# A relational graph network with attention: layers two and three gather three bf16 parts of each row instead of fp32 rows

## The chip, the cores and the metric

The kernel runs on one core of one Trainium2 chip. The metric is the device time of one execution in microseconds (us); of several runs the median is given. All engine times below come from one profiled execution.

A core has five engines with a queue of instructions each. TensorE multiplies matrices (PE in the profile; PEld is its loading of weights). VectorE (DVE) and ScalarE (ACT) work on elements. GpSimd (POOL) is used here almost only to issue gathers. SyncE (SP) issues ordinary DMAs. Each engine works through its queue in order and waits on semaphores for the others.

## The reference

A graph has 6250 nodes with 256 features and 100,000 edges (`src`, `dst`, sorted by `dst`), each with one of eight types. Three relational layers are followed by one attention layer, each of the two blocks with a residual and a layer norm:

```python
edge_index = jnp.stack([src, dst])
for l in range(3):                                   # relational block
    xr = jnp.einsum('nd,rde->rne', x, W_rel[l])      # 8 x 6250 x 256
    msg = xr[edge_type, src]
    agg = jax.ops.segment_sum(msg, dst, num_segments=x.shape[0])
    x = jax.nn.relu(agg + x @ W_root[l] + bias[l])
x = layernorm(x_in + x)
# attention block: logits from x @ weight, softmax over the heads, then
x = layernorm(x + attention(x))
```

All inputs and the output are fp32. The destinations are drawn as the square of a uniform number, so low node numbers have many more edges than high ones.

## The kernel before, in words

**Sums before weights.** A layer sums the raw rows of the source nodes first, separately for each destination node and edge type, and multiplies the sums with the eight weight matrices afterwards. Edges are cut into 782 tiles of 128. The first 36 tiles, whose destinations are the lowest nodes, are treated in another way (`count` and `products`); the other 746 tiles are gathered in every layer.

**Groups.** `Plan.order` puts the 746 tiles into 188 groups of four (three groups have two) and deals them to two streams, f = 0 for the high edge tiles and f = 1 for the low ones, mostly taking turns. Each stream runs from high nodes to low ones and has a ring `S[f]` in SBUF: four node tiles of 128 columns for f = 0, three for f = 1, for each of two feature halves and eight types.

**An iteration** of the loop in `layer` (L778) handles one group, in an order that is written out by hand:

- `gather` (L492) issues four indirect DMAs on POOL (L496). Each fetches 128 rows of 1 KB from the table of the layer into a tile `msg`. The pool `mp` has eight such buffers. The table of layer one is the input, those of layers two and three are `xs[1]` and `xs[2]` in DRAM.
- `onehot` (L476) makes, four groups ahead, the 0/1 matrix `oh` on VectorE (L480): for each edge, 1 in the column of its destination and type. `w` is eight times the width of the group's window of nodes, from 32 to 208 columns.
- `finish` (L593) handles a node tile whose products are done: VectorE adds the bias (L595), ScalarE applies the relu (L598), SP stores the rows to `xs[l + 1]` (L599). In the last layer it continues with residual and layer norm. `clear` (L589) then zeroes the tile's columns in the ring on ScalarE.
- `windows` (L501) multiplies `msg` with `oh` on TensorE, two products per edge tile (one for each half of the features), into a PSUM tile `pw` (L513). There are four such banks.
- Pieces of `dense` (L572) come next: two root products (L577) and sixteen relation products (L581) per node tile, all fp32, six of them in an iteration for each node tile in progress.
- `add` (L518) adds each window from PSUM into the ring at the place of its nodes (L525), on VectorE.
- A node tile whose last group has come is folded (L557, L559) and queued for `dense`. Tile 13 gets edges from both streams. Its sums from stream 1 are copied to `hold[13]` by `keep` (L565, ScalarE) and added later to the ring of stream 0 by VectorE (L824).

**Other work in the loop.** In layer one, from iteration 56, `count` (L633) makes two selection matrices an iteration on VectorE (L647) for the hot nodes. From iteration 130 `products` (L663) loads all rows again in tiles `msg`. In layer three `logits` (L619) transposes each finished tile and multiplies it, and from iteration 164 `prepare` (L703) readies the attention, also with tiles `msg`.

**The order of the layers.** A gather of a layer needs all rows of the layer before, so at each seam the last group, its dense products, the relu and the store all have to end before the first gather of the next layer starts. The weights of the next layer are loaded by ScalarE's queue at the same point (L228). `split3` (L877) is an existing helper that writes a tensor as three bf16 tensors with the same sum: a cast, a subtraction, a cast, a subtraction, a cast, on VectorE. It is used for two small tensors of the attention.

Of the kernel before, what the change touches and what calls it, by code (L numbers as in the profile page):

```python
# [20 lines left out]
P = 128  # L21
# [96 lines left out]
@with_exitstack  # L118
def kernel(
    ctx: ExitStack,  # L120
    tc: tile.TileContext,
    x: bass.AP,
    src: bass.AP,
    dst: bass.AP,
    edge_type: bass.AP,
    w_rel: bass.AP,
    w_root: bass.AP,
    bias: bass.AP,
    weight: bass.AP,
    attn_l: bass.AP,  # L130
    attn_r: bass.AP,
    out: bass.AP,
):
    nc = tc.nc
    N, D = x.shape
    E = src.shape[0]
    L, R = w_rel.shape[0], w_rel.shape[1]
    H, DH = attn_l.shape
    KC = D // P
    pl = Plan(N, E, R)  # L140
    NT, T, CH, WMAX = pl.NT, pl.T, pl.CH, pl.WMAX
    LAST = N - (NT - 1) * P
    assert R * WMAX * KC <= 512 and E >= NT * P and NT <= P

    const = ctx.enter_context(tc.tile_pool(name="const", bufs=1))
    dram = ctx.enter_context(tc.tile_pool(name="dram", bufs=1, space=DRAM))
    xs = [x] + [dram.tile([N, D], F32, name=f"x{l}") for l in range(1, L)]

    flag = const.tile([1, 1], I32, name="flag")

    fast(tc, const, pl, x, xs, src, dst, edge_type, w_rel, w_root, bias, weight,
         attn_l, attn_r, out, flag)

    bad = nc.values_load(flag[0:1, 0:1], min_val=0, max_val=6 * T)  # L154
    with tc.If(bad > 0):
        general(tc, x, src, dst, edge_type, w_rel, w_root, bias, weight, attn_l, attn_r, out)


def fast(tc, const, pl, x, xs, src, dst, edge_type, w_rel, w_root, bias, weight,
# [10 lines left out]
    with ExitStack() as top:  # L170
# [31 lines left out]
        with ExitStack() as s:  # L202
            wp = s.enter_context(tc.tile_pool(name="wp", bufs=1))
            sp = s.enter_context(tc.tile_pool(name="sp", bufs=1))
            mp = s.enter_context(tc.tile_pool(name="mp", bufs=8))
# [10 lines left out]
            hold = {j: sp.tile([P, KR, P], F32, name=f"hold{j}") for j in sorted(pl.shared(pl.TM))}  # L216
# [23 lines left out]
            with tc.manual_schedule():  # L240
                for l in range(L):
                    wr, wo = load_w(l)
                    opn = layer(
                        tc, pl, l, l == L - 1, groups, ready, S, hold, A, hk, hl, idx, key, pos,
                        iota, ident, wr, wo, bias_b, x, xs, eps, w1x, altab, y,
                        (al3, ga, hif, yT0, lane, dst, iota_p),
                        mp, op, xp, hp, ps_w, ps_d, ps_t, H)
# [194 lines left out]
def fold_weights(tc, mp, w1x, weight, attn_l, attn_r):  # L442
# [6 lines left out]
    for i, a in enumerate((attn_r, attn_l)):  # L449
        t = mp.tile([P, GT, D], F32, name="msg")  # L450
        ab, pr = t[:, 0], t[:, 1:1 + KC]
        nc.sync.dma_start(ab, a.rearrange("h d -> (h d)").partition_broadcast(P))
        nc.vector.tensor_tensor(pr, w1x[:, :, :D], ab.unsqueeze(1).to_broadcast([P, KC, D]),
                                ALU.mult)
        for k in range(KC):
            nc.vector.tensor_reduce(w1x[:, k, D + i * H:D + (i + 1) * H],
                                    pr[:, k].rearrange("p (h d) -> p h d", h=H), AX.X, ALU.add)


def layer(tc, pl, l, final, groups, ready, S, hold, A, hk, hl, idx, key, pos, iota, ident, wr, wo,  # L460
          bias_b, x, xs, eps, w1x, altab, y, att, mp, op, xp, hp, ps_w, ps_d, ps_t, H):
# [14 lines left out]
    def onehot(i):  # L476
        g = groups[i][1]
        w = R * pl.W[g[0] // WB]
        oh = op.tile([P, GT, R * pl.WMAX], F32, name="oh")
        nc.vector.tensor_tensor(  # L480
# [11 lines left out]
    def gather(i):  # L492
        g = groups[i][1]
        msg = mp.tile([P, GT, D], F32, name="msg")
        for q, t in enumerate(g):
            nc.gpsimd.indirect_dma_start(  # L496
                out=msg[:, q, :], out_offset=None, in_=table,
# [3 lines left out]
    def windows(i, msg, oh):  # L501
# [6 lines left out]
        for n, (q, t) in enumerate(reversed(list(enumerate(g)))):  # L508
# [3 lines left out]
            for k in range(KC):  # L512
                nc.tensor.matmul(pw[:, k * w:(k + 1) * w], msg[:, q, k * P:(k + 1) * P],  # L513
                                 oh[:, q, :w], start=True, stop=True)
# [50 lines left out]
    def keep(j):  # L565

        i = nc.scalar.copy(hold[j], cols(1, j))
        tc.add_to_no_dep_group(f"used{l}_1_{j}", i.ins)
        done[1].append(j)
        clear(1, j)  # L570

    def dense(f, j, xT):  # L572
# [3 lines left out]
        for k in range(KC):  # L576
            nc.tensor.matmul(pd[:, :D], xT[:, k], wo[:, k], start=(k == 0), stop=False)  # L577
            yield
        for k in range(KC):
            for r in range(R):  # L580
                i = nc.tensor.matmul(pd[:, :D], s[:, k * R + r], wr[:, k, r],  # L581
                                     start=False, stop=(k == KC - 1 and r == R - 1))
# [10 lines left out]
    def finish(j, pd):  # L593
        n = rows(j)
        nc.vector.tensor_tensor(pd[:, :D], pd[:, :D], bias_b[:, l], ALU.add)  # L595
        if not final:
            h = xp.tile([P, D], F32, name="h", bufs=2)
            nc.scalar.activation(h, pd[:, :D], AF.Relu)  # L598
            nc.sync.dma_start(xs[l + 1][j * P:j * P + n, :], h[:n])  # L599
            return  # L600
# [13 lines left out]
        yt = xp.tile([P, D], F32, name="yt", bufs=2)  # L614
# [48 lines left out]
    def products():  # L663
# [4 lines left out]
        def load(js):  # L668
            t = mp.tile([P, GT, D], F32, name="msg")
# [33 lines left out]
    def prepare():  # L703
# [8 lines left out]
        for m in range(len(parts) + 2):  # L712
            todo = []
            if m < len(parts):
                js = parts[m]
                t = mp.tile([P, GT, D], F32, name="msg")
# [12 lines left out]
            if m >= 2:  # L729
                js = parts[m - 2]  # L730
                t = mp.tile([P, GT, D], F32, name="msg").rearrange("p a d -> p (a d)")
# [46 lines left out]
    for i in range(NG + 5):  # L778
# [18 lines left out]
        for f, j, pd in fin:  # L797
            yt = finish(j, pd)
            clear(f, j)
            if final:  # L800
                log.append((i, (j, yt)))
# [16 lines left out]
        for f, j in sorted((k for k, r in ready.items() if r == i), key=lambda k: -k[1]):  # L818
            fold(f, j)
            if f == 1 and j in late:  # L820
                keep(j)
                continue
            if j in hold:
                nc.vector.tensor_tensor(cols(f, j), cols(f, j), hold[j], ALU.add)  # L824
            turned.append(dense(f, j, xTs.pop(j)))
# [507 lines left out]
```

## Time and profile before

| | |
|---|---|
| Median of 3 runs | 2999.32 us (2997.8 to 3003.55) |
| Profiled execution, its own time | 2994.72 us |
| Its span, first to last instruction | 2993.0 us |
| Mean granted TensorE clock | 0.933 |
| POOL busy | 2159.9 us, 2238 gathers of 0.95 us |
| PE busy | 2667.7 us |
| VectorE busy | 1667.6 us |
| Software DMA queue (the gathers) | 293.48 MB, 33.7% of the time of 16 DMA engines |

A busy share is an average over stages. An instruction that issues a DMA from SP or ACT doesn't count as busy, but an indirect gather on POOL does. "L513" is line 513 of the kernel. A row of the groups reads: line, engine, operation, output and inputs with the number of instructions; then busy time and the mean of one; then idle time of the engine just before them and what ended it. In the timeline a row gives start, time, engine, line, operation, and in brackets the idle time before it. An fp32 matmul appears as two records.

### The profile page before, as it was taken

The page shows a single profiled execution, that of the slowest core. Times are in us where ns is not written, and L with a number is a line of the kernel's source. Part 1 is how long each engine was busy: PE and PEld are TensorE (multiplying, and loading weights), DVE is VectorE, ACT ScalarE, POOL GpSimd, SP SyncE. Part 2 cuts the span into 40 slices and gives each one's busy share as a digit, 9 for nine tenths or more (in the row PEclk, how much of TensorE's full clock was granted, in tenths as well). Part 3 has the DMA queues.
Part 4 walks back from the last instruction along what each step waited for, and adds up shares of the span by engine and source line. Part 5 has one row for each costly group of instructions (what it writes and reads, how often), then busy time and mean ns, then how long its engine had stood idle before and what let it go on. Part 6 is the DMA issues. An engine that isn't in the chain of part 4 may idle for free. (4 is left out here: it accounts for less than half of the span.)

```text
span 2993.0 us, 45318 instructions
## 1 busy us (share of the span) xinstructions
PE 2667.7 (89%) x15710; PEld 2424.1 (81%) x15711; DVE 1667.6 (56%) x4106; ACT 462.6 (15%) x611; POOL 2159.9 (72%) x2258
## 2 busy tenths in 40 slices
PE   5999999999987799999998997789999999999874
PEld 4989888888876798998887887678888888898763
DVE  7655667754433555554444443355656655555775
ACT  2111111111001111111111010011111111111015
POOL 6777777777775777777777777577777777777723
PEclk9999999999878899999999997799999999999885
DMA  5444444445433344444434543344444444454634
GB/s 153 125 123 122 119 123 120 120 133 170 135 116 115 117 123 122 125 123 118 123 116 146 164 126 117 117 119 131 126 132 128 125 127 127 150 169 138 187 97 131
DMA packets 203053, 388.97 MB, mean 130 GB/s; under 512 B 42885, under 2 KB 128004, under 8 KB 202820
## 3 DMA queue, kind: packets, MB, share of 16 engines
q0 software_dynamic: 107424, 293.48, 33.7%
q1 hardware_dynamic: 87464, 85.04, 8.9%
q10 hardware_dynamic: 7932, 7.48, 0.7%
q8 instruction: 130, 2.13, 0.3%
q14 instruction: 103, 0.84, 0.1%
HBM read 360.18 MB, written 25.65 MB: 129 GB/s over the span
## 5 line engine op out<-in xcount | busy, mean ns | idle before, releaser
L496 POOL DMA_INDIRECT msg<-x,idx x1492 | 1419.2, 951 | 504.6 <-issue 411.9
L513 PE MATMUL pw<-oh,msg 128*128 128x160 f32 (+22 forms) x8952 | 1308.0, 303 | 195.6 <-DMA msg<-x,idx 101.4
L513 PEld LDWEIGHTS pw<-oh,msg 128*128 128x128 f32 x8952 | 1253.8, 202 | 261.2 <-issue 119.9
L525 DVE TENSOR_TENSOR S<-S,pw 128x320 f32 (+22 forms) x2238 | 904.5, 404 | 989.4 <-PE pd L581 508.1
L581 PE MATMUL pd<-wr,S 128*128 128x256 f32 x4704 | 1107.0, 385 | 1.7 <-DVE S L525 1.4
L581 PEld LDWEIGHTS pd<-wr,S 128*128 128x128 f32 x4704 | 893.1, 193 | 119.3 <-DVE S L525 3.6
L496 POOL DMA_INDIRECT msg<-in_x_dram,idx x746 | 709.0, 950 | 236.0 <-issue 210.8
L480 DVE TENSOR_TENSOR oh<-iota,key 128x640 f32<-128x640 f32 (+23 forms) x564 | 363.8, 647 | 26.4 <-issue 14.8
L590 ACT ACTIVATE S<-S 128x2048 uint32<-128x2048 uint32 x150 | 285.0, 1900 | 0.1
L551 ACT COPY xT<-pt 128x256 f32<-128x256 f32 x195 | 72.3, 371 | 972.6 <-PE pt L548 972.5
L598 ACT ACTIVATE h<-pd 128x256 f32<-128x256 f32 x98 | 37.7, 384 | 937.0 <-DVE pd L595 752.3
L577 PE MATMUL pd<-wo,xT 128*128 128x256 f32 x588 | 168.3, 412 | 3.3 <-ACT h L598 3.3
L595 DVE TENSOR_TENSOR pd<-pd,bias_b 128x256 f32<-128x256 f32 x147 | 63.1, 429 | 172.4 <-PE pd L581 172.3
L577 PEld LDWEIGHTS pd<-wo,xT 128*128 128x128 f32 x588 | 110.0, 205 | 13.1 <-ACT h L598 3.7
L647 DVE TENSOR_SCALAR sel<-iota,hk 128x392 bf16<-128x392 f32 x138 | 80.4, 613 | 0.0
L612 ACT ACTIVATE rs<-mv,eps 128x1 f32<-128x1 f32 x49 | 14.4, 295 | 413.1 <-DVE mv L611 413.1
L685 PE MATMUL pd<-msg,A 128*128 128x256 f32 x294 | 71.5, 386 | 1.5 <-DMA msg<-x 1.5
L1014 POOL TENSOR_TENSOR z<-yg,td 128x1536 f32<-128x1536 f32 (+1 forms) x9 | 29.3, 3268 | 56.7 <-DVE bn L992 28.0
L685 PEld LDWEIGHTS pd<-msg,A 128*128 128x128 f32 x294 | 55.7, 196 | 8.5 <-issue 1.8
L548 PE MATMUL pt<-ident,xin 128*128 128x128 f32 x294 | 57.4, 278 | 1.4 <-ACT xT L551 1.4
L629 PEld LDWEIGHTS pt<-w1x,xT 128*128 128x128 f32 x192 | 25.8, 195 | 35.2 <-ACT xT L551 35.2
L548 PEld LDWEIGHTS pt<-ident,xin 128*128 128x128 f32 x294 | 41.2, 145 | 12.7 <-ACT xT L551 2.4
(187 smaller groups left out, 669.4 us busy)
## 6 DMA issues: line engine op xcount, KB each, us to landing
msg<-x,idx POOLq DMA_INDIRECT x1492, 2.7
x<-h SPq DMA_DIRECT2D x96, 128.0 KB
xin<-x SPq DMA_DIRECT2D x96, 128.0 KB
msg<-x SPq DMA_DIRECT2D x24, 512.0 KB
msg<-in_x_dram,idx POOLq DMA_INDIRECT x746, 2.7
y<-yt SPq DMA_DIRECT2D x49, 128.0 KB
wr<-in_L_gnn_W_rel_dram ACTq DMA_DIRECT2D x6, 1024.0 KB
xin<-in_x_dram SPq DMA_DIRECT2D x48, 128.0 KB
```

The source lines that it names most:

```text
L480: nc.vector.tensor_tensor(oh[:, :len(g), :w], iota[:, :w].unsqueeze(1).to_broadcast([P, len(g), w]), key[:, g[0]:g[-1] + 1].unsqueeze(2).t ...
L496: nc.gpsimd.indirect_dma_start(out=msg[:, q, :], out_offset=None, in_=table, in_offset=bass.IndirectOffsetOnAxis(ap=idx[:, t:t + 1], axis=0))
L513: nc.tensor.matmul(pw[:, k * w:(k + 1) * w], msg[:, q, k * P:(k + 1) * P], oh[:, q, :w], start=True, stop=True)
L525: ins = nc.vector.tensor_tensor(o, o, pw.rearrange("p (a b) -> p a b", b=W), ALU.add)
L548: nc.tensor.transpose(pt[:, k * P:(k + 1) * P], t[:, k * P:(k + 1) * P], ident)
L551: nc.scalar.copy(xT.rearrange("p k n -> p (k n)"), pt[:, :D])
L577: nc.tensor.matmul(pd[:, :D], xT[:, k], wo[:, k], start=(k == 0), stop=False)
L581: i = nc.tensor.matmul(pd[:, :D], s[:, k * R + r], wr[:, k, r], start=False, stop=(k == KC - 1 and r == R - 1))
L590: i = nc.scalar.memzero(cols(f, j))
L595: nc.vector.tensor_tensor(pd[:, :D], pd[:, :D], bias_b[:, l], ALU.add)
L647: nc.vector.tensor_scalar(oh, iota[:, :NT * R], float(512 * n), hk[:, t:t + 1], op0=ALU.add, op1=ALU.is_equal)
L685: nc.tensor.matmul(ph[:, :D], A[:, j], t[:, n], start=(n == 0), stop=(j == js[-1]))
```

## The change

- **A second table.** Beside `xs[l]` there is `xb[l]` for layers two and three, with rows of 1536 bytes. `finish` of layers one and two splits the relu's result with `split3` into three bf16 parts, stored side by side, and stores the tile there with a further DMA on SP.
- **Gathers.** Layers two and three gather rows of `xb[l]`. The `msg` tile grows from 4 x 1 KB to 4 x 1.5 KB per partition, in all layers, and the pool `mp` has six buffers instead of eight.
- **Products of edge tiles.** In layers two and three `windows` runs three bf16 products, summed in PSUM, in place of each fp32 one. The one-hot matrix is written as bf16 there, in the same buffer. Layer one keeps fp32.
- **The shared node tile.** `keep` goes. Tile 13 now runs `dense` for stream 1 as well, without root products, and `finish` copies the result (256 columns) from PSUM to `hold[13]`. When stream 0 finishes the tile, this is added to its PSUM result. This holds for all three layers.

```diff
+    xb = [None] + [dram.tile([N, 3 * D // 2], F32, name=f"xb{l}") for l in range(1, L)]
...
-            mp = s.enter_context(tc.tile_pool(name="mp", bufs=8))
+            mp = s.enter_context(tc.tile_pool(name="mp", bufs=6))
...
-            hold = {j: sp.tile([P, KR, P], F32, name=f"hold{j}") for j in sorted(pl.shared(pl.TM))}
+            hold = {j: sp.tile([P, D], F32, name=f"hold{j}") for j in sorted(pl.shared(pl.TM))}
...
         oh = op.tile([P, GT, R * pl.WMAX], F32, name="oh")
+        if l:
+            oh = oh.rearrange("p g w -> p (g w)").bitcast(BF16)[:, :GT * R * pl.WMAX].rearrange(
+                "p (g w) -> p g w", g=GT)
...
-        msg = mp.tile([P, GT, D], F32, name="msg")
+        msg = mp.tile([P, GT, 3 * D // 2], F32, name="msg")
         for q, t in enumerate(g):
             nc.gpsimd.indirect_dma_start(
-                out=msg[:, q, :], out_offset=None, in_=table,
+                out=msg[:, q, :] if l else msg[:, q, :D], out_offset=None, in_=xb[l] if l else table,
...
             for k in range(KC):
-                nc.tensor.matmul(pw[:, k * w:(k + 1) * w], msg[:, q, k * P:(k + 1) * P],
-                                 oh[:, q, :w], start=True, stop=True)
+                if l == 0:
+                    nc.tensor.matmul(pw[:, k * w:(k + 1) * w], msg[:, q, k * P:(k + 1) * P],
+                                     oh[:, q, :w], start=True, stop=True)
+                    continue
+                m3 = msg[:, q].bitcast(BF16)
+                for c in range(3):
+                    nc.tensor.matmul(pw[:, k * w:(k + 1) * w],
+                                     m3[:, c * D + k * P:c * D + (k + 1) * P], oh[:, q, :w],
+                                     start=(c == 0), stop=(c == 2))
...
-    def keep(j):
-
-        i = nc.scalar.copy(hold[j], cols(1, j))
-        tc.add_to_no_dep_group(f"used{l}_1_{j}", i.ins)
-        done[1].append(j)
-        clear(1, j)
-
     def dense(f, j, xT):
...
-        for k in range(KC):
+        for k in range(KC if xT is not None else 0):
             nc.tensor.matmul(pd[:, :D], xT[:, k], wo[:, k], start=(k == 0), stop=False)
...
-    def finish(j, pd):
+    def finish(f, j, pd):
         n = rows(j)
+        if f == 1 and j in late:
+
+            nc.vector.tensor_copy(hold[j], pd[:, :D])
+            return
+        if j in hold:
+            nc.vector.tensor_tensor(pd[:, :D], pd[:, :D], hold[j], ALU.add)
         nc.vector.tensor_tensor(pd[:, :D], pd[:, :D], bias_b[:, l], ALU.add)
         if not final:
             h = xp.tile([P, D], F32, name="h", bufs=2)
             nc.scalar.activation(h, pd[:, :D], AF.Relu)
             nc.sync.dma_start(xs[l + 1][j * P:j * P + n, :], h[:n])
+            t = xp.tile([P, 3 * D // 2], F32, name="yt", bufs=2)
+            split3(nc, xp, t.bitcast(BF16).rearrange("p (c d) -> p c d", c=3), h)
+            nc.sync.dma_start(xb[l + 1][j * P:j * P + n, :], t[:n])
             return
...
             fold(f, j)
-            if f == 1 and j in late:
-                keep(j)
-                continue
-            if j in hold:
-                nc.vector.tensor_tensor(cols(f, j), cols(f, j), hold[j], ALU.add)
-            turned.append(dense(f, j, xTs.pop(j)))
+            kept = f == 1 and j in late
+            turned.append(dense(f, j, None if kept else xTs.pop(j)))
```

The helper that is called for the split, unchanged by the diff:

```python
def split3(nc, pool, o, v):

    r = pool.tile(list(v.shape), F32, name="rest", bufs=1)
    nc.vector.tensor_copy(o[:, 0], v)
    nc.vector.tensor_tensor(r, v, o[:, 0], ALU.subtract)
    nc.vector.tensor_copy(o[:, 1], r)
    nc.vector.tensor_tensor(r, r, o[:, 1], ALU.subtract)
    nc.vector.tensor_copy(o[:, 2], r)
```

## The prediction

> **What bounds the kernel now.** I read the page's busy shares and costliest groups first, then the stretches, then the timeline at the seams between layers.
>
> ```profile
> PE 2667.7 (89%) x15710; PEld 2424.1 (81%) x15711; DVE 1667.6 (56%) x4106; ACT 462.6 (15%) x611; POOL 2159.9 (72%) x2258
> L496 POOL DMA_INDIRECT msg<-x,idx x1492 | 1419.2, 951 | 504.6 <-issue 411.9
> ```
>
> TensorE looks like the bound and GpSimd (POOL) looks 28% free. The second line corrects that: a gather is 951 ns, and most of POOL's idle time is "issue", not a wait for another engine. The table of stretches settles it (columns: stretch; length; PE, PEld, DVE, ACT, POOL busy with counts; clock; DMA).
>
> ```profile
> 300.00:400.00 100.00, 94.39 (x566) 84.48 (x565) 71.39 (x162) 16.12 (x20) 75.63 (x81) 1.00 0.42 123
> 1100.00:1200.00 100.00, 97.44 (x556) 89.12 (x556) 53.19 (x105) 17.52 (x20) 75.63 (x81) 1.00 0.42 123
> 1800.00:1900.00 100.00, 83.96 (x443) 76.71 (x444) 34.42 (x101) 7.67 (x9) 76.21 (x79) 0.76 0.38 112
> ```
>
> PE goes from 97 to 84 busy and its clock from 1.00 to 0.76, while POOL stays near 76. In the timeline gathers start every 1.25 us: 0.95 of instruction and 0.30 between. A layer has 746 gathers, so 746 x 1.25 = 932 us, and the spans from first to last gather are 936.0, 935.3 and 947.6 us. **The pace of gathers is the bound**; PE is a close second that sets the time in three places only: where POOL waits for a message buffer that PE still reads, at the seams, and at the end. Counting matmuls against gathers in the timeline, the third layer loses 14.7 us to gathers that start late (PE runs up to seven groups behind there), the first 3.4 and the second 2.8.
>
> The seam between layers one and two:
>
> ```profile
> 946.02 0.95 POOL L496 DMA_INDIRECT msg<-in_x_dram,idx  x1 [0.31 <-issue]
> ...
> 953.61 7.17 PE L581 MATMUL pd<-wr,S 128*128 128x256 f32 x32
> 960.89 0.43 DVE L595 TENSOR_TENSOR pd<-pd,bias_b 128x256 f32<-128x256 f32 x1 [7.33 <-PE pd L581]
> 961.36 0.38 ACT L598 ACTIVATE h<-pd 128x256 f32<-128x256 f32 x1 [7.78 <-DVE pd L595]
> 967.16 0.94 POOL L496 DMA_INDIRECT msg<-x,idx  x1 [20.19 <-DMA wr<-in_L_gnn_W_rel_dram]
> ```
>
> POOL stands still for 20.19 us. The line names the weight load, but what the gather needs is the last stored row: relu ends at 961.74 and store and completion take 5.4 us.
>
> **The Trainium skill.** "SBUF — State Buffer", section "Who interferes with whom", says that a VectorE cast in its two-port mode locks GpSimd out of the shared SBUF port. The new split has three casts, so this decides whether POOL slows. The trace has the same five operations once, beside gathers:
>
> ```profile
> 2762.39 0.27 DVE L880 CAST al<-altab 128x196 bf16<-128x196 f32 x1
> 2762.70 0.36 DVE L881 TENSOR_TENSOR rest<-altab,al 128x196 f32<-128x196 f32 x1
> 2762.89 0.99 POOL L496 DMA_INDIRECT msg<-x,idx  x1 [0.30 <-issue]
> 2763.79 0.26 DVE L884 CAST al<-rest 128x196 bf16<-128x196 f32 x1
> 2764.18 0.95 POOL L496 DMA_INDIRECT msg<-x,idx  x1 [0.30 <-issue]
> ```
>
> The gather beside them took 0.99 instead of 0.95 and the next started 0.04 late: the lock, if taken, costs little here. "TensorE: Matmul & The Clock Gate", section "Weight-path perf modes — Fast Weight Load (FWL) and DoubleRow", says that non-fp32 weights of 128 columns load fast; the trace agrees (192 ns per fp32 LDWEIGHTS record, 98 for the bf16 ones of L742). "DMA: Bandwidth & Descriptors", section "SWDGE vs HWDGE vs iDMA", says that GpSimd builds one descriptor pair per DMA operation. A row stays one contiguous piece, so the number of pairs should not grow; no gather here has another row size, so the trace can't confirm it.
>
> **The parts.**
>
> 1. *Edge products of layers two and three (L513).* An fp32 product shows as two records, so a tile has four, then six bf16 ones.
>
> ```profile
> 2777.88 1.18 PE L742 MATMUL pw<-al,A 128*128 128x196 bf16 x12
> 2779.06 1.95 PE L513 MATMUL pw<-oh,msg 128*128 128x40 f32 x16
> ```
>
> Twelve bf16 matmuls of 196 columns take about 84 ns each from start to start; short ones (L965 with L969) pair up at 87 ns, 43 each. Narrow tiles go from 4 x 112 = 0.45 us to 6 x 43 = 0.26, tiles of 168 columns from 4 x 143 = 0.57 to about 6 x 72 = 0.43. So 0.14 to 0.19 a tile, some 250 us of PE over 1492 tiles, nearly all beside POOL's pace. What of it lies on the path: of the third layer's 14.7 us of late gathers, 8.1 fall before iteration 150, where PE is behind because of the extra transposes and logits, and 6.6 in the last 17 iterations, where buffers are shared with the attention preparation. A group of four saves about 0.6 us and PE's lag there grew by 22 us over 48 groups, so the lag goes; I count 9 back. At the ends of layers two and three PE is 1.9 and 4.3 us behind the last data; about 2 each.
>
> 2. *Bytes of a gather, 128 to 192 KB.* The software queue takes 33.7% of the DMA engines, 1008 us for 2238 gathers, 0.45 us of each 1.25. Times 1.5 that is 0.68; with the other queues' tenth the engines stay below 0.8. POOL's own 0.95 us: I take it as unchanged. Bounds: 5% less, or in proportion to bytes, 50% more.
>
> 3. *Six message buffers instead of eight.* A gather of group i waits for the products of group i-6. In the timeline of layer one this distance is negative only at group 8 (-2.7 us), and small at groups 88 to 90 (1.1, 0.9, 0.6 us). Layer two has at least 10 us everywhere. By itself: +2.7.
>
> 4. *Split for layers one and two, 98 node tiles.* Casts: 0.18 us at 28 elements and 0.27 at 196 give about 0.30 at 256; subtractions, from 0.19 and 0.36, about 0.42. Sum 3 x 0.30 + 2 x 0.42 + gaps = 1.9 us, and VectorE must first wait for the relu (0.4). Behind these 2.3 us stand the adds L525 of that iteration, and PE waits for the adds when all four window banks are full. In layer one PE has no slack: from group 11 to 90 it is 8 to 23 us behind its data, so what it loses stays lost. Mostly the 2.8 us of dense pieces hide the delay; from iteration 56 to about 127 VectorE also builds selections (1.2 us an iteration, 71% busy) and PE already waits for adds. I take 0.2 us for 13 tiles and 1.0 for 12 up to group 90: about 15. Bounds 0 and 2.3 each, so 0 to 57, though the upper one would need VectorE to be late every time.
>    POOL: 0.04 us x 98 = 4, of which 3 count. Stores: xb is 98 more SP DMAs (192 KB); loads queued behind on SP wait about 2 us, with three iterations of slack.
>
> 5. *Tile 13 multiplied twice.* The copy of S (ACT) and the 128x2048 add (DVE) go, off the path. Sixteen fp32 products come, 32 records, 7.2 us by the 953.61 line, at groups 9 to 11 of each layer. In layers two and three the savings of part 1 absorb it. In layer one it stays as lag.
>
>    Parts 3 to 5 meet in layer one at group 90: 7.2 + 15 - 0.6 left of distance = **+21**; as VectorE catches up in some iterations I take 16 (7 with a free split, 30 with a bad one).
>
> 6. *Seams.* The split adds 1.9 us behind the relu. The bigger store: 128 KB moved in 1.0 us beside the weight load, 192 KB in 1.5. So +2.4 at each of two seams. PE's 2 us cancel one of them, unless the half clock seen when PE starves stretches the final 7.2 us; I add 1 for that.
>
> The bf16 one-hots (L480) still read fp32 from PSUM: the same time, off the path.
>
> Sum: layer one +16, casts +3, seams +4.8 + 1 - 2, third layer -9, its end -2: **+12 us**. The profiled execution took 2994.7 (span 2993.0); 2994.7 + 12 = 3006.7. The median of the runs, 2999.3, lies 4.6 above that execution, so 3011.
>
> **Rivals.**
>
> *Faster, by relief.* If dense pieces hide every split, layer one loses only the few us that buffers and tile 13 make certain; if these too are caught up between groups, what is left is the seams (+4 to 5) against all the late gathers of layer three and its end (-14.7 and -4): 2985 to 2990. It decides where POOL loses under 5 us in layer one (5 + 3 + 4.8 - 18.7 is -6). For it: PE's weight loads waited for adds only 22 us of 580 there. Against: the distances of 0.6 to 1.1 us at groups 88 to 90. Chance 0.07.
>
> *Faster, because PE is the bound.* 250 us of PE would go: about 2750. Against: POOL's constant pace. 0.02.
>
> *Gathers cost more with bytes.* 2% of 1.25 us x 1492 is 37 us (3048), 10% 187 us, and a POOL instruction in proportion to bytes 0.48 x 1492 = 710 us (3720). Nothing in the trace speaks against it, as all rows are alike. 0.13.
>
> *The change acts as said*: its instruction list has three bf16 products for each fp32 one, so I keep no case for that.
>
> **Numbers.** The main case has 0.78, own range 2995 to 3035, likeliest 3011; about 0.21 of it lies within 0.2% (6 us, about what a measurement of this kernel can tell from no change). Range 2990 to 3050: it leaves out the deep end of the first rival, PE as bound, and expensive gathers. Faster 0.09, same 0.21, slower 0.7.
>
> **What would show it.** Right: gathers of layers two and three still 0.95 us at 1.25 us; first layer longer by 10 to 25 us with POOL waiting for PE near groups 60 to 100; second layer within 4 us of 935; third near 938; seams about 22 to 24 us; PE busy down by 200 to 250 us. Wrong: a gather over 0.97 us, a first layer within 4 us of 936, or waits of gathers on PE in layer two.

## The result, and the profile after

The changed kernel takes 3036.71 us (median of 4 runs, 3033.82 to 3040.61) against 3000.55 for the kernel before on the same chip: a ratio of 1.0121, 95% interval 1.0104 to 1.0139. It is **slower by 36 us**, or 1.2%. The profiled execution took 3040.61 us (span 3038.9, mean TensorE clock 0.907), 45.9 more than the profiled one of before. Of these 46, about 10 lie in how the two executions stand to their medians (one 3.9 above, the other 5.8 below), so the parts below add up to 46 and not to 36.

The busy shares, the gathers, the bf16 products and the software queue on the page of the changed kernel:

```profile
PE 2474.7 (81%) x18790; PEld 2179.8 (72%) x18791; DVE 1836.3 (60%) x4599; ACT 456.2 (15%) x608; POOL 2163.4 (71%) x2258
q0 software_dynamic: 131296, 391.26, 44.5%
L501 POOL DMA_INDIRECT msg<-xb,idx x1492 | 1419.3, 951 | 523.6 <-issue 427.6
L524 PE MATMUL pw<-oh,msg 128*128 128x40 bf16 (+19 forms) x8952 | 607.4, 228 | 342.9 <-DMA msg<-xb,idx 293.0
```

PE lost 193 us of work, VectorE gained 169, and a gather costs POOL 951 ns with 1.5 KB rows as with 1 KB rows. So PE was relieved and the time still rose. (The edge products of layers two and three alone fell from 874 to 607 us; other work took 73 back, 37 of it the relation products of `dense`, which has 96 records more for tile 13.) The same three stretches (columns: stretch; length; PE, PEld, DVE, ACT, POOL busy with counts; clock; DMA):

```profile
300.00:400.00 100.00, 93.79 (x535) 84.08 (x534) 76.94 (x176) 15.37 (x18) 72.60 (x78) 0.97 0.42 129
1100.00:1200.00 100.00, 94.45 (x760) 83.02 (x758) 69.37 (x146) 17.89 (x21) 75.94 (x80) 1.00 0.65 189
1800.00:1900.00 100.00, 64.08 (x639) 55.37 (x640) 45.47 (x126) 9.40 (x10) 75.63 (x81) 0.82 0.61 176
```

POOL falls below its 76 in the first row only, which is layer one. The DMA share rises to 0.65 in layer two and POOL's pace doesn't mind. To find the time I again measured from the first to the last gather of each layer in the timelines:

| us | before | after | difference | predicted |
|---|---|---|---|---|
| layer one | 936.0 | 958.8 | +22.8 | +19 (16, and 3 for casts) |
| seam one to two | 20.2 | 26.8 | +6.6 | seams together +3.8 |
| layer two | 935.3 | 937.8 | +2.5 | 0 |
| seam two to three | 20.6 | 22.3 | +1.7 | (above) |
| layer three | 947.6 | 956.0 | +8.4 | -9 |
| from the last gather to the end | 122.3 | 126.1 | +3.8 | -2 |

The start before the first gather is 0.2 longer; together +46. Layer three is where the forecast has the wrong sign. Its late gathers (what is beyond 1.25 us from the start of one gather to the next) changed in two opposite ways: up to group 164 they fell from 8.1 to 2.1 us, after it they rose from 6.6 to 21.6. Four lines of the timeline in that last stage (start, length, instruction, [idle before, releaser]):

```profile
2868.35 2.58 PE L524 MATMUL pw<-oh,msg 128*128 128x120 bf16 x24 [5.41 <-DMA msg<-xb,idx]
...
2871.20 0.94 POOL L501 DMA_INDIRECT msg<-xb,idx  x1 [4.34 <-PE pw L524]
...
2888.30 0.94 POOL L501 DMA_INDIRECT msg<-xb,idx  x1 [3.55 <-DVE A L741]
...
2897.11 0.95 POOL L501 DMA_INDIRECT msg<-xb,idx  x1 [4.12 <-issue]
```

PE waits 5.4 us for data, then POOL's gather waits 4.3 us for these products: in this stage neither sets the pace, they wait for each other around a ring of buffers that is too short (e1 and e6 test this). The third line names who else holds the ring: the attention preparation (`prepare`, L741 here), which takes its tiles from the same pool `mp`.

The seam between layers one and two:

```profile
968.97 0.94 POOL L501 DMA_INDIRECT msg<-in_x_dram,idx  x1 [0.30 <-issue]
...
978.33 0.29 DVE L894 CAST yt<-rest 128x256 bf16<-128x256 f32 x1
978.54 0.99 DVE L537 TENSOR_TENSOR S<-S,pw 128x64 f32 x4
...
979.58 7.17 PE L586 MATMUL pd<-wr,S 128*128 128x256 f32 x32 [1.62 <-DVE S L537]
986.80 0.43 DVE L606 TENSOR_TENSOR pd<-pd,bias_b 128x256 f32<-128x256 f32 x1 [7.27 <-PE pd L586]
987.31 0.38 ACT L609 ACTIVATE h<-pd 128x256 f32<-128x256 f32 x1 [8.79 <-issue]
987.73 0.30 DVE L890 CAST yt<-h 128x256 bf16<-128x256 f32 x1 [0.50 <-ACT h L609]
...
989.31 0.29 DVE L894 CAST yt<-rest 128x256 bf16<-128x256 f32 x1
...
996.73 0.95 POOL L501 DMA_INDIRECT msg<-xb,idx  x1 [26.82 <-DMA wo<-in_L_gnn_W_root_dram]
```

The split stands here twice. From relu's end to the first gather it is now 9.04 instead of 5.42 us (+3.6): 1.9 us are the split, and from its end to the gather it takes 7.1 us, 1.7 more than before from relu's end. The line names a weight load again, but the gather needs the rows of `xb`, as it needed those of `xs` before. And the split of the node tile before, which ends at 978.62, stands ahead of the last adds (978.54) on VectorE, so the last dense products start late: PE had been idle for 1.62 us, against 0.14 before. That is half of the 3.0 us by which relu ends later against the last gather. The other half is that PE stands further behind by then: its last products of edge tiles start 5.2 us after the start of the pause instead of 3.7.

### The profile page after: what moved, and what is told of

Read it like the earlier page. It is cut to its first block, busy times and chain, and to the rows that moved or that the text cites. A ratio compares the mean times of both kernels' runs of the same rounds, so it can differ in the third digit from the quotient of the medians.

```text
span 3038.9 us, 51628 instructions
## 1 busy us (share of the span) xinstructions
PE 2474.7 (81%) x18790; PEld 2179.8 (72%) x18791; DVE 1836.3 (60%) x4599; ACT 456.2 (15%) x608; POOL 2163.4 (71%) x2258
## 3 DMA queue, kind: packets, MB, share of 16 engines
q0 software_dynamic: 131296, 391.26, 44.5%
## 4 chain that ended last, share of the span: by engine, by line
PE 47%; POOL 18%; issue 12%; DMA 12%; DVE 7%; ACT 2%; DVEq 0%; ACTq 0%; POOLq 0%; SPq 0%
PE pd L586 23%; POOL msg L501 17%; DMA msg<-xb,idx 10%; PE pw L519 9%; PE pw L524 8%; DVE S L537 4%; PE pd L582 3%; PE pd L699 1%; DMA msg<-in_x_dram,idx 1%; ACT o L1042 1%; PE pt L560 1%; PE pt L643 1%; DVE sel L661 1%; ACT xT L563 0%; DVE oh L485 0%
## 5 line engine op out<-in xcount | busy, mean ns | idle before, releaser
L501 POOL DMA_INDIRECT msg<-xb,idx x1492 | 1419.3, 951 | 523.6 <-issue 427.6
L586 PE MATMUL pd<-wr,S 128*128 128x256 f32 x4800 | 1143.6, 389 | 26.1 <-DVE S L537 24.7
L586 PEld LDWEIGHTS pd<-wr,S 128*128 128x128 f32 x4800 | 916.2, 195 | 152.9 <-DVE S L537 32.3
L524 PE MATMUL pw<-oh,msg 128*128 128x40 bf16 (+19 forms) x8952 | 607.4, 228 | 342.9 <-DMA msg<-xb,idx 293.0
L524 PEld LDWEIGHTS <-msg 128*128 128x128 bf16 x8952 | 553.7, 104 | 416.0 <-DMA msg<-xb,idx 339.8
L519 PE MATMUL pw<-oh,msg 128*128 128x160 f32 (+22 forms) x2984 | 435.6, 303 | 60.3 <-DVE S L537 31.2
L519 PEld LDWEIGHTS pw<-oh,msg 128*128 128x128 f32 x2984 | 417.1, 203 | 90.4 <-DVE S L537 42.8
L485 DVE TENSOR_TENSOR oh<-iota,key 128x640 bf16<-128x640 f32 (+40 forms) x564 | 364.2, 647 | 29.4 <-issue 18.1
L582 PE MATMUL pd<-wo,xT 128*128 128x256 f32 x588 | 178.7, 432 | 3.2 <-ACT h L609 3.2
L890 DVE CAST yt<-h 128x256 bf16<-128x256 f32 x98 | 30.5, 311 | 49.8 <-ACT h L609 49.3
```

The source lines that it names most:

```text
L485: nc.vector.tensor_tensor(oh[:, :len(g), :w], iota[:, :w].unsqueeze(1).to_broadcast([P, len(g), w]), key[:, g[0]:g[-1] + 1].unsqueeze(2).t ...
L501: nc.gpsimd.indirect_dma_start(out=msg[:, q, :] if l else msg[:, q, :D], out_offset=None, in_=xb[l] if l else table, in_offset=bass.Indire ...
L524: nc.tensor.matmul(pw[:, k * w:(k + 1) * w], m3[:, c * D + k * P:c * D + (k + 1) * P], oh[:, q, :w], start=(c == 0), stop=(c == 2))
```

## The experiments

The first eight ran on two chips, beside the kernel before at 2998 us (e1 to e4) and 3000 us (e5 to e8). Layers, seams and ends are measured as above, each against the profile of before shown there. Profiles are single executions and differ from their medians by up to 10 us, so parts are read from the profiles and totals from the ratios. e5 to e7 are compared with the changed kernel on another chip, by way of the ratios.

**e1: six buffers and nothing else.**

```diff
-            mp = s.enter_context(tc.tile_pool(name="mp", bufs=8))
+            mp = s.enter_context(tc.tile_pool(name="mp", bufs=6))
```

> The kernel before with six message buffers instead of eight, nothing else. Theory 1 (GpSimd's pace is the bound, and what the change loses it loses where a gather waits for a buffer): layer one +3 to +6 us, layer two +0 to +1, layer three +20 to +25 (about 10 from PE's lag of up to seven groups in the middle, about 14 in the last 25 iterations, where the attention preparation shares the buffers); in all about +25, 3025 us. Theory 2 (VectorE's split and the longer seams cost the time, buffers are incidental): within 3 us of before. Theory 3 (the gathers' bytes cost it): within 3 us of before.

Measured: 3033.89 us, ratio 1.0115 (1.0098 to 1.0132). Layer three +31.9 (some 22 of it after group 164, 10 before), layer one +5.3, seams and layer two within 0.5. POOL's waits for PE in before and in e1 (engine, tile and line, releaser: us in total, times, longest):

```profile
POOL msg L496 <- PE pw L513: 32.6, 98, 1.4
```

```profile
POOL msg L496 <- PE pw L513: 72.3, 117, 5.8
```

**This one line costs as much as the whole change.** The prediction had it at +2.7, and theory 1 at +25: that theory held, with more lost in layer three than it gave. The 5.3 us of layer one are a single wait, group 4, which the changed kernel shows too:

```profile
31.30 0.40 DVE L458 TENSOR_REDUCE w1x<-msg 128x4 f32<-128x256 f32 x1
...
31.97 1.37 POOL L501 DMA_INDIRECT msg<-in_x_dram,idx  x1 [5.94 <-DVE hk L387]
```

A preparation for the attention (`fold_weights`) takes two buffers of `mp` ahead of group 0. With six, the gathers of group 4 get the first of these. VectorE, which has much else to do there, reads it in L458 until 31.70, and the gather starts 0.06 us after the end of L387 (31.91), which follows on VectorE.

**e2: e1 and tile 13 multiplied twice.**

```diff
-            hold = {j: sp.tile([P, KR, P], F32, name=f"hold{j}") for j in sorted(pl.shared(pl.TM))}
+            hold = {j: sp.tile([P, D], F32, name=f"hold{j}") for j in sorted(pl.shared(pl.TM))}
...
-            if f == 1 and j in late:
-                keep(j)
-                continue
...
+            kept = f == 1 and j in late
+            turned.append(dense(f, j, None if kept else xTs.pop(j)))
```

> As the previous kernel, and tile 13 multiplied twice instead of its sums being copied. Theory 1: PE is 7.2 us later from group 11 of layer one on, and with only 0.6 us of distance left at group 90 GpSimd loses 6 to 8 us there; in layer three, where PE is late too, 5 to 8 more; layer two unchanged. In all 12 to 16 us above the kernel with six buffers alone, about 3040. Theory 2 or 3: no change against the kernel with six buffers.

Measured: 3041.59 us, 1.0137 (1.0120 to 1.0153), some 8 us more than e1 (the longest execution of e1 is 3037.2 us, the shortest of e2 3037.8). That is about half of what was expected. Layer one 941.1 against e1's 941.3: nothing, a miss. The seams took 1.7 and 1.9 more than in e1, layer three 4.4, the end 2.0. The extra products do put PE 6 us further behind than before from group 16 to 48 of layer one (7.2 in the changed kernel), but POOL doesn't have to wait for it there or at group 90.

**e3: the changed kernel, but layers two and three still gather fp32 rows and multiply in fp32.** The split and its store are made and not read.

```diff
-                out=msg[:, q, :] if l else msg[:, q, :D], out_offset=None, in_=xb[l] if l else table,
+                out=msg[:, q, :D], out_offset=None, in_=table,
...
-                if l == 0:
+                if True:
                     nc.tensor.matmul(pw[:, k * w:(k + 1) * w], msg[:, q, k * P:(k + 1) * P],
```

> The changed kernel, but layers two and three still gather the fp32 rows and multiply in fp32: six buffers, tile 13 twice, the split and the extra store stay (the split rows are stored and not read). Theory 1: layer one as in the changed kernel, 957 to 960 us from first to last gather; seams of about 27 and 27 us; layer three as in the kernel with six buffers and tile 13. In all 22 to 30 us above that kernel, about 3068, and 30 above the changed kernel, since the bf16 products do relieve PE in layer three. Theory 2: most of the loss appears only here, all of +36 or more over before, and the changed kernel is about the same as this one. Theory 3 (bytes): this kernel is faster than the changed one by 10 us or more.

Measured: 3065.92 us, 1.0219 (1.0196 to 1.0241). The split and its store cost 24 us over e2 in the medians (13 in the profiles: layer one +11.8, layer two +5.9, layer three 5.8 less). The five executions of e3 spread from 3054.6 to 3071.6 us and the profiled one is near the lower end, so about 11 of the 24 us are not located. In layer one the waits of PE for VectorE's adds show it. In the stretch 300 to 640 of e2, then of the changed kernel, whose layer one is that of e3 (e3 has 16.5 and 24.8 us there). PE and PEld are two records of one engine, so the two lines show the same waits and are not added up:

```profile
PE pw L513 <- DVE S L525: 5.1, 11, 1.6
PEld pw L513 <- DVE S L525: 12.3, 18, 2.0
```

```profile
PE pw L519 <- DVE S L537: 16.4, 16, 2.6
PEld pw L519 <- DVE S L537: 24.7, 21, 3.0
```

Either line grows by 11 to 12 us, about as much as layer one. The seams didn't move (22.2 and 22.5 against 22.4 and 22.8), where 27 had been expected: the gathers of e3 need only the fp32 store, which goes out ahead of the split. In layer two e3, with fp32 rows, takes 939.8 us and the changed kernel 937.8, so the bytes of the larger rows cost nothing that can be seen.

**e4: the changed kernel again**, on this chip, as the end of the series.

> The changed kernel itself, for its time beside the other three on the same chip. All theories: 1.010 to 1.014 of before.

Measured: 3037.11 us, 1.0123 (1.0106 to 1.0139). Against e3 the bf16 parts give back 29 us in the medians; in the profiles it is 20.9 in layer three, while the first seam takes 5.0 more. So the sum of the whole, by the ratios: six buffers +34, tile 13 +7, split +25, bf16 products -29: +37.

e4's layer one took 959.6 us and e3's 952.9, though the code of layer one is the same. The difference shows in the windows from 520 to 560 us, first of the changed kernel, then of e3 (the clock is the third number from the end):

```profile
520.00:560.00 40.00, 35.27 (x184) 31.56 (x183) 31.41 (x74) 5.86 (x8) 27.66 (x30) 0.83 0.40 119
```

```profile
520.00:560.00 40.00, 34.97 (x218) 30.80 (x217) 34.43 (x82) 5.86 (x8) 30.26 (x33) 1.00 0.44 129
```

PE is as busy in both lines and gets through 184 instead of 218 instructions. In the profiles of after and of e4, two executions of one kernel, the granted clock drops to between 0.66 and 0.78 in the same two stretches of 10 us there, and PE falls 6 to 7 us further behind (26.7 against 20.7 us at group 104). In e3 and e6 it stays at 1.00 there. Why was not settled. About 6 of layer one's +22.8 go with this drop, and not with the split.

**e5: the split after the adds.** If the split costs by standing ahead of the adds, it should cost little at the end of the iteration.

```diff
-            split3(nc, xp, t.bitcast(BF16).rearrange("p (c d) -> p c d", c=3), h)
-            nc.sync.dma_start(xb[l + 1][j * P:j * P + n, :], t[:n])
+            later.append((j, n, h))
...
             turned.append(dense(f, j, None if kept else xTs.pop(j)))
+        for j, n, h in later:
+            t = xp.tile([P, 3 * D // 2], F32, name="yt", bufs=2)
+            split3(nc, xp, t.bitcast(BF16).rearrange("p (c d) -> p c d", c=3), h)
+            nc.sync.dma_start(xb[l + 1][j * P:j * P + n, :], t[:n])
+        later.clear()
```

> The changed kernel with the split and its store issued at the end of the iteration, behind the adds of the windows, instead of ahead of them. Theory 1a (in layer one it is the adds held up behind the split that make PE late; the changed kernel's PE loses 26 us there between groups 48 and 120): PE's extra lag falls from 33 to under 15 us, layer one from 959 to 944 to 949 us, and each seam is about 1.5 us shorter; in all 12 to 18 us below the changed kernel, about 3022. Theory 1b (VectorE simply has too much to do in the selection stage, the order doesn't matter): layer one stays at 955 to 960, in all 0 to 4 us below.

Measured: 3054.72 us, 1.0177 (1.0162 to 1.0192). **A miss**: layer one grew to 969.5 us and layer two to 945.5. The waits of PE's weight loads in the stretch 300 to 640:

```profile
PEld pw L519 <- DVE S L537: 19.7, 18, 4.0
PEld pw L519 <- issue: 8.2, 12, 2.1
PEld pd L582 <- ACT h L609: 6.8, 4, 3.7
```

The waits for adds fell a little (19.7 instead of 24.7 us), but those for the relu of a finished tile rose from 3.6 to 6.8, and those that end in "issue" from 2.6 to 8.2. At the end of an iteration the split stands ahead of the next iteration's selections, bias and adds, and VectorE is 76% busy in this stretch. That this is the whole cause was not shown.

**e6: seven buffers.** The room comes from one buffer of one-hots less.

```diff
-            mp = s.enter_context(tc.tile_pool(name="mp", bufs=6))
-            op = s.enter_context(tc.tile_pool(name="op", bufs=AHEAD + 2))
+            mp = s.enter_context(tc.tile_pool(name="mp", bufs=7))
+            op = s.enter_context(tc.tile_pool(name="op", bufs=AHEAD + 1))
```

> The changed kernel with seven message buffers, for which one of the six one-hot buffers is given up. Theory 1: the late gathers of the last 25 iterations fall from 22 us to 3 to 8, as a gather there then waits for products of two or three groups back and not for the preparation's own tiles; layer one 3 to 6 us shorter. In all 18 to 24 us below the changed kernel, about 3017. Rival (what is lost there comes from the preparation's work on VectorE, which seven buffers don't lighten): at most 6 us below.

Measured: 3033.08 us, 1.0109 (1.0094 to 1.0124); its interval overlaps that of the changed kernel, and the total is the one that the rival gave. The wait at group 4 is gone (layer one's loss up to group 10 is 1.4 instead of 6.2 us), and the stage after group 164 still loses 17.2 us instead of 21.6 to 23.1. POOL's waits there, from 2780 to 2915 us:

```profile
POOL msg L501 <- DVE A L741: 11.2, 5, 4.6
POOL msg L501 <- PE pw L524: 4.0, 1, 4.0
```

In the changed kernel it was 13.9 us for PE and 3.5 for L741. With seven buffers gathers wait mostly for the preparation's own tile, not for PE. Its selection matrices are built by VectorE behind the adds, so a buffer lent to it comes back late. One buffer more turns most of one wait into the other.

**e7: both**, the seven buffers of e6 and the late split of e5.

```diff
-            mp = s.enter_context(tc.tile_pool(name="mp", bufs=6))
+            mp = s.enter_context(tc.tile_pool(name="mp", bufs=7))
...
+            later.append((j, n, h))
```

> The two previous edits together. Theory 1: they act at different places, so their gains add: 30 to 40 us below the changed kernel, 2998 to 3007, within 0.3% of the kernel before. Rival (both remove waits of the same gathers): no more than the better one of the two.

Measured: 3045.00 us, 1.0154 (1.0139 to 1.0168). Layer one 963.4, the stage after group 164 17.1 again. That is 12 us more than e6, the second miss for the late split, so both theories fell.

**e8: the kernel before with nine buffers** (and one one-hot buffer less). Would more than eight have paid?

```diff
-            mp = s.enter_context(tc.tile_pool(name="mp", bufs=8))
+            mp = s.enter_context(tc.tile_pool(name="mp", bufs=9))
```

> The kernel before with nine message buffers instead of eight, for which one of the six one-hot buffers is given up; none of the change. Theory 1: layer three loses 14.7 us to late gathers before, of which 5 to 9 come back; the rest is the same: 2989 to 2994, 0.2 to 0.3% faster. Rival (eight are enough, the late gathers have another cause): within 2 us of before.

Measured: 3002.68 us, 1.0011 (1.0003 to 1.0018). No gain: layer three's loss from group 10 to 130 fell from 4.4 to 1.7 us, that from 130 to 164 rose from 3.7 to 7.6. So the step from eight to nine, paid for with a one-hot buffer, is worth nothing, and that from eight to six costs 34 us.

**The last four** ran on a chip where the kernel before itself takes 3650.39 us (75 runs). Gathers still last 0.95 us there, but POOL stands still about 2 us longer at intervals that are mostly 11.9 us (median; some 200 such pauses in the profile of e10, about 2 us on average), as here in e10:

```profile
389.86 0.94 POOL L496 DMA_INDIRECT msg<-in_x_dram,idx  x1 [2.23 <-PE pt L548]
...
401.79 0.95 POOL L496 DMA_INDIRECT msg<-in_x_dram,idx  x1 [2.22 <-PE pd L581]
```

What makes these pauses the profile doesn't show; the named releasers are not what the gathers need, and VectorE starts little in them either. A layer takes 1111 to 1177 us there. These four can be compared with one another and with their own kernel before, not with the runs above.

**e9: the changed kernel with eight large buffers**, one-hots two groups ahead.

```diff
-AHEAD = 4
+AHEAD = 2
...
-            mp = s.enter_context(tc.tile_pool(name="mp", bufs=6))
-            op = s.enter_context(tc.tile_pool(name="op", bufs=AHEAD + 2))
+            mp = s.enter_context(tc.tile_pool(name="mp", bufs=8))
+            op = s.enter_context(tc.tile_pool(name="op", bufs=AHEAD + 1))
```

> The changed kernel with eight message buffers of 1.5 KB rows; the room comes from the one-hots, built two groups ahead instead of four, in three buffers instead of six. Theory 1 (what the changed kernel loses in the preparation stage of layer three, 22 to 23 us, is the shared ring of message buffers being too short): with eight, as in the kernel before, that stage loses about 7 again, and layer one is as short as with seven buffers or shorter (946 to 950 us). 3037 - 15 - 11 = about 3011, ratio 1.002 to 1.007. Rival (seven buffers left 17 us there because PE and VectorE themselves are late, not the ring): the stage still loses 15 or more, 3022 to 3028, ratio 1.007 to 1.010. If one-hots two groups ahead cost something, the next kernel shows it.

**e10: the kernel before with one-hots two groups ahead**, the control for e9.

```diff
-AHEAD = 4
+AHEAD = 2
...
-            op = s.enter_context(tc.tile_pool(name="op", bufs=AHEAD + 2))
+            op = s.enter_context(tc.tile_pool(name="op", bufs=AHEAD + 1))
```

> The kernel before with one-hots two groups ahead in three buffers, eight message buffers as before: the control for the run with eight large buffers. A one-hot takes 0.3 to 0.6 us of VectorE and two groups are 5 us of gathers, so the short lead costs nothing or little: 2998 to 3004, ratio within 0.002. Rival: the lead covers VectorE's long stretches (the run with nine buffers and a lead buffer less had its loss in groups 130 to 164 of layer three rise from 3.7 to 7.6 us): 5 to 12 us slower.

Measured: e9 1.0039 (1.0023 to 1.0056), e10 0.9987 (0.9970 to 1.0004). The short lead costs nothing that can be seen (a one-hot took 0.65 us on average before, more than the 0.3 to 0.6 written there). e9's ratio is the one that the ring theory expected, but it doesn't settle the matter: after group 164 of layer three e9 loses 52.1 us and its control 54.0, while e11, with six buffers, loses 43.5. The pauses cover what the test was to show. Whether eight large buffers would bring the stage back to before is therefore open.

**e11: the three casts on ScalarE.**

```diff
-    nc.vector.tensor_copy(o[:, 0], v)
+    nc.scalar.copy(o[:, 0], v)
...
-    nc.vector.tensor_copy(o[:, 1], r)
+    nc.scalar.copy(o[:, 1], r)
...
-    nc.vector.tensor_copy(o[:, 2], r)
+    nc.scalar.copy(o[:, 2], r)
```

> The changed kernel with the three casts of the split on ScalarE (15% busy) instead of VectorE; the subtractions stay. Theory A (the adds are delayed by the time that VectorE is busy with the split): VectorE does 0.86 us a node tile instead of 1.8, layer one's late gathers of groups 56 to 130 halve from 14 to 7 us, 3028 to 3032, ratio 1.009 to 1.011. Rival B (they are delayed by how long the chain relu, cast, subtract, cast, subtract holds VectorE, which takes its instructions in order): a ScalarE cast takes about 0.38 us, like the relu, and four changes of engine come in, so VectorE is held about as long, 2.3 us and more; layer one is the same or up to 8 us longer, the seams 0.5 to 1 us longer: 3037 to 3047, ratio 1.012 to 1.016. I hold B for the likelier.

Measured: 1.0025 (1.0007 to 1.0042); the changed kernel was not run on that chip, so the ratio alone doesn't choose between the theories. The timeline says how long VectorE is held:

```profile
336.39 0.43 DVE L606 TENSOR_TENSOR pd<-pd,bias_b 128x256 f32<-128x256 f32 x1 [2.04 <-PE pd L586]
336.86 0.38 ACT L609 ACTIVATE h<-pd 128x256 f32<-128x256 f32 x1 [7.32 <-issue]
337.27 0.41 ACT L890 CAST yt<-h 128x256 bf16<-128x256 f32 x1
337.71 0.42 DVE L891 TENSOR_TENSOR rest<-h,yt 128x256 f32<-128x256 f32 x1 [0.89 <-ACT h L609]
338.17 0.40 ACT L892 CAST yt<-rest 128x256 bf16<-128x256 f32 x1 [0.49 <-issue]
338.60 0.42 DVE L893 TENSOR_TENSOR rest<-rest,yt 128x256 f32<-128x256 f32 x1 [0.47 <-ACT yt L892]
```

From the end of the bias (336.82) to the end of the last subtraction (339.02) VectorE gives 2.2 us to the split, 0.85 of it working; it starts nothing else in between. That is also the median of the 98 node tiles; with the casts on VectorE it is 2.5. Moving 0.9 us of work away frees 0.3 us of the queue, because VectorE takes its instructions in order and so gives away the waits inside the chain too (0.89 and 0.47 us in these lines). This part of rival B is shown. What it did to the whole time is not: the ratios that A and B expected (1.009 to 1.016) were worked out from runs without the pauses.

**e12: bf16 parts for layer three alone**, eight buffers, one-hots two groups ahead; layer one neither splits nor stores parts.

```diff
-                out=msg[:, q, :] if l else msg[:, q, :D], out_offset=None, in_=xb[l] if l else table,
+                out=msg[:, q, :] if final else msg[:, q, :D], out_offset=None, in_=xb[l] if final else table,
...
-                if l == 0:
+                if not final:
...
+            if l == 0:
+                return
```

> Bf16 parts for layer three alone: layer one stores fp32 rows only and layer two gathers them and multiplies in fp32, as before; layer two splits, layer three gathers parts. Eight message buffers, one-hots two groups ahead. Theory (the split hurts where PE has no slack, in layer one, and six buffers hurt in the preparation stage): layer one within 3 of 936, first seam 20 to 22.5, layer two 935 to 940, second seam 22 to 24, layer three 938 to 943, tail 125 to 127: 2996 to 3003, ratio 0.999 to 1.001. Rival (large buffers or the short lead cost something of their own, or layer two has no room for the split beside fp32 products): 3005 to 3015, ratio 1.002 to 1.005.

Measured: 1.0017 (1.0000 to 1.0034), against 0.9987 of the control e10: between the two theories, and no gain. Its interval overlaps those of e9 and e11, so it isn't shown to be milder than the whole change is on that chip. No version of the change was faster than the kernel before.

## Why the prediction was right, and where it was not

The predicted time was 3011 and the measured 3036.7. The sign was right for a good reason: what the change relieves lies beside POOL's pace, and what it adds lies partly on it. The size was not. The sum of +12 stands against +46 in the profiles (+36 in the medians). The time lies outside the main case's own range (2995 to 3035), and that the wider one (to 3050) held is luck of its width. Of the signs that it named, layer three near 938 us, the first seam at 22 to 24 and PE 200 to 250 us down did not come (956.0, 26.8 and 193). Step by step:

- **The pace of gathers bounds, and bytes don't change it** (part 2): right. 951 ns, 1.25 us pitch, with the software queue at 44.5% instead of 33.7%. The queue moves 64 instead of 48 packets for a gather of layers two and three, and POOL's time for it is the same. PE's relief bought back late gathers of layer three only, and the rivals "PE is the bound" and "gathers cost more with bytes" fell.
- **Relief of layer three's middle** (part 1): right in mechanism. Late gathers up to group 164 fell by 6.0 us of the 8.1 counted there.
- **The last stage of layer three** (parts 1 and 3): this is the largest miss. Part 1 expected that its 6.6 us would shrink with faster products; they grew by 15. Part 3 measured the distance between a gather and the products of group i-6 in layers one and two, and never in the stage where other code draws from the same pool. The term "by itself +2.7" was 34 us in e1. That the shortage there is of the shared pool is shown by e1 (only the number of buffers differs) and by e6's waits for tile A. Why seven buffers still lose 17.2 us there and eight in the kernel before only 6.6 is not separated from the rest of the change.
- **Group 4 of layer one**: +5.4, not foreseen, also from part 3: the two buffers that `fold_weights` takes ahead of the loop were not counted.
- **The split in layer one** (part 4): the forecast of 15 us up to group 90 compares with e2 to e3's 11.8 in the whole layer, but the distribution was wrong. Up to group 48 the split cost nothing (PE's lag was flat at 7.2, tile 13 alone); it grew only where the selections of `count` share VectorE, from 7 to 16 us by group 88. That +19 came near the +22.8 is luck: group 4 (5.4) and the drop of the clock (6), which it didn't have, stand in for tile 13 (7), which cost nothing there (e2).
- **Seams** (part 6): +8.3 instead of +3.8. The split cost 1.9 us, as forecast, but the larger store 1.7 at the first seam instead of 0.5: from relu's end to the first gather it takes 3.6 and 3.0 us more instead of 2.4. The split of the tile before holds the last adds, so that PE idles 1.6 us ahead of the last dense products at both seams. And e2, without any split, has seams 1.7 and 1.9 us longer than e1, from tile 13, for which part 5 had put nothing at the seams. What the faster products save shows at the second seam, where these dense products start 5.5 instead of 6.7 us after the last gather.
- **The end**: -2 was expected, +3.8 came. The products do end 3.3 us earlier against the last gather, but the final dense then waits for adds that stand behind tile 13's new add and the norm of the tile before, so it starts only 0.5 us earlier; and it runs slower, by 2.5 us. The first line is before, the second after:

```profile
2880.33 7.17 PE L581 MATMUL pd<-wr,S 128*128 128x256 f32 x32 [0.61 <-DVE S L525]
```

```profile
2921.96 9.68 PE L586 MATMUL pd<-wr,S 128*128 128x256 f32 x32 [3.40 <-DVE S L537]
```

The same 32 matmuls took 7.17 us at a granted clock of 1.00 and 9.68 us at 0.74. The prediction had named a slower clock after starving as a risk of 1 us at a seam; it came here, at the end (at the first seam, after 1.62 us of idling, they took 7.17). The remaining 1.8 us are in the attention behind it and are not explained.

One sum of the prediction doesn't come out: the -6 of the first rival makes 2993, not 2985 to 2990. No later step rests on it.

## What to carry to other kernels

Before a pool is made smaller, list everything that draws from it, over the whole program and also ahead of the loop, and check the distance to the release in the stage where the borrowers are slowest, not in the stage that is easiest to measure. Work saved on an engine that waits for another's pace is worth only the late starts that it caused there (14.7 us in layer three of the kernel before, and 29 us in e4 against e3, where six buffers had made more of them), while fewer buffers and a longer chain at a seam are paid in full. A chain of small operations put ahead of others on an in-order engine holds it for its whole length, the waits in it too, and how much of that reaches the end differed from stage to stage here, so price it stage by stage.

## What was not expected of the hardware

- A gather of 128 rows of 1.5 KB takes POOL 951 ns, as one of 1 KB rows does; the DMA share of layers two and three went from about 0.4 to 0.6 and the pitch stayed at 1.25 us.
- The granted clock fell to between 0.66 and 0.78 in two stretches of 10 us in the middle of layer one in both profiles of the changed kernel and stayed at 1.00 there in e3, whose layer one has the same instructions; layer one was 6 to 7 us longer with it.
- On one chip the same program took 3650 instead of 3000 us, by pauses of about 2 us in intervals of mostly 11.9.
- The casts of the split took 0.29 us alone and 0.32 on average. The prediction named what the Trainium skill ("SBUF — State Buffer", section "Who interferes with whom") says on the port that VectorE's casts share with GpSimd. Gathers of layers one and two that run beside a subtraction of the split average 1.00 us, against 0.95 for the rest, 8 us in all over the two layers. But in e11, whose casts are on ScalarE, they still average 0.98 us, so VectorE's casts are not the whole reason; what else is wasn't settled. Layer one's gathers average 955 ns against 950 in the kernel before, about 3 us over the layer, as allowed for.
